# A convolution cut into single taps, an expert choice in four parts, and PSUM places opened earlier, in the last stage of a two-layer kernel

## The chip, the cores and the metric

The kernel runs on one core of a Trainium2 chip, in one launch, in fp32 throughout. The metric is the device time of an execution in microseconds; each kernel has the median of several executions, and one more execution is taken with the hardware profiler. All rows below are from that profiled execution.

The engines are named as the profile names them: PE (matmuls; PEld are its weight loads), DVE (VectorE), ACT (ScalarE), POOL (GpSimd) and SP (which issues DMAs). A matmul writes its result to PSUM, which is used here in eight places of 128 x 512 fp32; DVE or ACT reads it from there and so frees the place.

## What is computed

Two layers on `x` (2 x 1024 tokens of 256), with a context of 2 x 77 tokens. Every part is added to `x`.

```python
x = x + L0_xattn(ctx, layernorm(x))      # context and tokens as keys, 16 heads of 64
x = x + L0_ffn(layernorm(x))             # 8 experts of width 1024, 2 per token, layernorm behind
x = x + L1_xattn(layernorm(x), ctx, ctx) # 16 heads of 16 over 77 keys, causal mask
x = x + L1_ffn(layernorm(x))             # below
```

The change lies in the last line. With `h` for the normalized tokens it is

```python
scores = sigmoid(h @ Wr)                      # 8 choices, 4 of them expert networks
idx = top_k(scores + router_bias, 2)
cw = scores at idx, divided by their sum, 0 elsewhere
routed = sum over e < 4 of cw[:, e] * ((silu(h @ Wg[e]) * (h @ Wu[e])) @ Wd[e])
routed += (cw[:, 4] + cw[:, 6]) * h + cw[:, 7] * relu(h)
shared = conv(h, conv_w) + conv_b             # per channel, 4 taps back in time
out = x + routed + shared
```

## The kernel before

The whole is one program of some 25,000 instructions, written out without loops at run time. The order of each engine's instructions is the order in which the Python code issues them (`manual_schedule`), and every engine takes its own queue strictly in that order. So an instruction that waits holds up all behind it on its engine.

The last stage runs through **steps** k = 0 to 49. Steps 0 to 31 are the attention of the second layer: step k scores one tile of 128 tokens for one half of the heads (`score` on PE, `soften` on DVE and an Exp on ACT), and in step k + 1 its result is turned on PE (`turn_step`) and copied out by ACT. Steps 0 to 19 are woven into the last experts of the first layer (two steps in each of their slots 29 to 38); steps 20 to 49 stand alone. `step(k)` issues, in this order: `pre` (projections, turns back, divides of tiles), the scores, `mid` (attend), the turns of the step before, soften. After it the lists `rest`, `fill` and `after` of this k are run, each in the order in which things were put into it.

The last feed-forward part is done by `Mix` for four **blocks** of 512 tokens. For a block, with k = 8 * blk + 13:

- `measure` (fill, k): mean and variance of four tiles on DVE, and the power -0.5 on POOL.
- `values` (fill, k + 1): nb on DVE, then four ACT instructions that write the normalized tiles.
- `turns` (fill, k + 2): eight PE transposes, two ACT copies.
- `choose`, in three parts (fill k + 3, after k + 3, fill k + 4): 16 matmuls of 8 columns and an Exp; then 8 small DVE instructions, which end with the first choice; then 14 more (lines 200 to 206 and 1481 to 1489), which give `cw`.
- four experts, two steps each, from step 19 on: `up` (rest, first step) has 8 matmuls of 512 columns into two PSUM places and a Tanh (in the last block a Silu) on ACT; its `product` on DVE is put into `after` of that step. `down` (rest, second step of the next expert) has 8 matmuls into two places, and DVE adds the four tiles of them, times `cw`, to `xr` (line 1584).
- `copies` (fill, second steps of the first two experts): four ACT and four POOL instructions for `h` and relu of `h`.
- the convolution: `convolve_first` (fill, second step of expert 0: 19, 27, 35, 43) has two ACT passes with the first tap; `convolve(c)` (fill, first steps of experts 1 and 2) has three taps on DVE for half c of the channels; `convolved` (rest, both steps of expert 3) turns the result with PE and adds it on DVE (line 1531).

The experts of blocks 0 to 3 begin at steps 19, 26, 34 and 42 (the two steps of the very first fall together).

The profile's starts of some steps on PE: step 18 at 1520.6 us, 22 at 1551.9, 23 at 1557.5, 24 at 1567.3, 31 at 1616.0, 33 at 1632.1, 34 at 1637.9, 40 at 1660.4, 42 at 1669.1.

PSUM in this stage: `ps_t` has three places that all turns, projections and small matmuls take in turn. `ps_h` has two, for `up`. `ps_o` has one, for `attend` and for the first two tiles of `down`. The last two places hold the scores (`ps_s`). While `ps_x` is None, the last two tiles of `down` take a place of `ps_t`. At step K3 = 42 the scores' places are given up, and `ps_x` is opened in them, with one place for every third matmul result of `up` and one for the last two tiles of `down`. Its tiles wait for the readers of the tile that was in the place before (`reuse_waits="tile"`).

```python
ups[0] += 1
pool = ps_x if ps_x is not None and ups[0] % 3 == 0 else ps_h
```

## Time and profile before

| | us |
|---|---|
| median of 3 executions | 1699.35 (1698.52 to 1704.48) |
| profiled execution | 1698.73 |
| its span, from the first to the last instruction | 1696.9 |
| PE busy in it | 1631.6 |
| DVE busy | 1092.3 |
| ACT busy | 708.4 |
| POOL busy | 853.0 |
| one tap of the convolution (line 1521), 24 of them | 0.74 to 1.30, median 1.04 |
| one ACT pass of the first tap (line 1508), 8 of them | 0.80 |
| one addition of `down` on DVE (line 1584), 64 of them | 0.48 |

How to read the views: the list of waits gives, for an engine and a line, what ended its idle time, then the us in total, the number of times and the longest. The timeline gives the start and length of an instruction or a run of like ones, in us, and in brackets the idle time before it with what ended it. The chain of waits gives start, length and instruction along the chain that ended last. The table by stretches gives the busy us of each engine, with the granted clock of PE behind them (1.00 is full speed).

### The profile page before, as it was taken

The page shows a single profiled execution, that of the slowest core. Times are in us where ns is not written, and L with a number is a line of the kernel's source. Part 1 is how long each engine was busy: PE and PEld are TensorE (multiplying, and loading weights), DVE is VectorE, ACT ScalarE, POOL GpSimd, SP SyncE. Part 2 cuts the span into 40 slices and gives each one's busy share as a digit, 9 for nine tenths or more (in the row PEclk, how much of TensorE's full clock was granted, in tenths as well). Part 3 has the DMA queues.
Part 4 walks back from the last instruction along what each step waited for, and adds up shares of the span by engine and source line. Part 5 has one row for each costly group of instructions (what it writes and reads, how often), then busy time and mean ns, then how long its engine had stood idle before and what let it go on. Part 6 is the DMA issues. An engine that isn't in the chain of part 4 may idle for free.

```text
span 1696.9 us, 25161 instructions
## 1 busy us (share of the span) xinstructions
PE 1631.6 (96%) x9368; PEld 1048.2 (62%) x9368; DVE 1092.3 (64%) x2169; ACT 708.4 (42%) x1405; POOL 853.0 (50%) x538
## 2 busy tenths in 40 slices
PE   8998999999999999999999999989999999999998
PEld 4544555555555555565555555457899987886655
DVE  5766766666666666767767776664522266666777
ACT  1544444444544444444443444451222135445542
POOL 1277656775676666755776766823040143222112
PEclk8999999999999999999999999999999999999999
DMA  3011222222211210000000000018888987530000
GB/s 120 25 50 63 75 68 69 75 69 69 75 69 63 81 69 7 7 20 1 13 13 7 7 20 29 1 50 304 308 282 297 325 291 224 166 99 20 13 13 25
DMA packets 124910, 151.95 MB, mean 90 GB/s; under 512 B 13259, under 2 KB 112757, under 8 KB 124789
## 3 DMA queue, kind: packets, MB, share of 16 engines
q1 hardware_dynamic: 80032, 102.18, 18.2%
q10 hardware_dynamic: 41685, 39.77, 6.7%
q0 software_dynamic: 3072, 8.39, 1.4%
q8 instruction: 75, 1.23, 0.3%
q14 instruction: 46, 0.38, 0.1%
HBM read 105.10 MB, written 45.22 MB: 89 GB/s over the span
## 4 chain that ended last, share of the span: by engine, by line
PE 72%; DVE 13%; ACT 6%; POOL 6%; issue 2%; DMA 1%; ACTq 0%; DVEq 0%; POOLq 0%
PE sc L758 13%; PE ptr L810 12%; PE po L835 8%; PE ph L1258 8%; PE po L1277 7%; PE pqk L688 6%; POOL pa L792 5%; DVE nm L768 5%; ACT pa L769 4%; PE pv L664 3%; PE py L703 3%; PE pg L1540 2%; PE ptr L1356 1%; PE sb L733 1%; ACT pT L124 1%
## 5 line engine op out<-in xcount | busy, mean ns | idle before, releaser
L792 POOL TENSOR_SCALAR pa<-pa,f 128x1024 f32<-128x1024 f32 x244 | 694.9, 2865 | 360.5 <-ACT pT L124 258.1
L769 ACT ACTIVATE pa<-sc,nm 128x1024 f32<-128x1024 f32 x256 | 282.9, 1109 | 427.6 <-DVE nm L768 424.5
L768 DVE TENSOR_REDUCE nm<-sc 128x1 f32<-128x1024 f32 x256 | 301.2, 1218 | 136.2 <-PE sc L758 136.2
L810 PE MATMUL ptr<-ident,pa 128*128 128x128 f32 x2048 | 285.3, 278 | 26.7 <-DVE kT L128 6.2
L810 PEld LDWEIGHTS ptr<-ident,pa 128*128 128x128 f32 x2048 | 224.9, 141 | 110.1 <-issue 61.4
L835 PE MATMUL po<-pT,v 128*64 128x512 f32 (+1 forms) x1152 | 262.6, 598 | 0.0
L758 PE MATMUL sc<-kT,qT 64*128 64x512 f32 x1024 | 257.1, 621 | 0.0
L128 DVE COPY pT<-ptr 128x512 f32<-128x512 f32 x256 | 175.4, 688 | 100.3 <-PE ptr L810 97.0
L124 ACT COPY pT<-ptr 128x512 f32<-128x512 f32 (+1 forms) x320 | 177.5, 587 | 135.2 <-PE ptr L810 131.8
L835 PEld LDWEIGHTS po<-pT,v 128*64 128x64 f32 (+1 forms) x1152 | 78.5, 136 | 153.8 <-issue 148.7
L1258 PE MATMUL ph<-xT,w 128*128 128x128 f32 x1248 | 150.0, 277 | 2.3 <-DVE xT L128 1.5
L1258 PEld LDWEIGHTS ph<-xT,w 128*128 128x128 f32 x1248 | 146.3, 194 | 5.2 <-DVE xT L128 2.2
L758 PEld LDWEIGHTS sc<-kT,qT 64*128 64x128 f32 x1024 | 89.2, 187 | 84.1 <-issue 80.8
L1277 PE MATMUL po<-w,hT 128*128 128x256 f32 x624 | 141.1, 379 | 0.0
L1277 PEld LDWEIGHTS po<-w,hT 128*128 128x128 f32 x624 | 115.5, 190 | 14.1
L1271 DVE TENSOR_SCALAR hT<-ph,bs 128x128 f32<-128x128 f32 x156 | 43.9, 344 | 102.5 <-PE ph L1258 95.3
L162 POOL TENSOR_TENSOR rstd<-ve,neghalf 128x1 f32<-128x1 f32 (+2 forms) x45 | 31.9, 710 | 152.2 <-DVE ve L155 128.9
L1269 ACT ACTIVATE hT<-ph,bs 128x128 f32<-128x128 f32 x156 | 44.3, 367 | 114.1 <-PE ph L1258 102.4
L1015 POOL DMA_INDIRECT yt<-tab_y,pos x32 | 31.5, 984 | 95.2 <-PE po L1277 80.9
L688 PE MATMUL pqk<-kvT,wk 128*128 128x512 f32 (+1 forms) x192 | 73.5, 513 | 0.0
L664 PE MATMUL pv<-wv,kvT 128*128 128x256 f32 (+1 forms) x288 | 69.2, 382 | 2.9 <-DVE pB L744 2.3
L664 PEld LDWEIGHTS pv<-wv,kvT 128*128 128x128 f32 (+1 forms) x288 | 52.3, 185 | 25.1 <-issue 16.2
(258 smaller groups left out, 1830.1 us busy)
## 6 DMA issues: line engine op xcount, KB each, us to landing
w<-in_L_ffn_W_dram SPq DMA_DIRECT2D x78, 1024.0 KB, 6.8
tab_x<-zero ACTq DMA_DIRECT2D x32, 512.0 KB, 3.2
tab_y<-zero ACTq DMA_DIRECT2D x32, 512.0 KB, 3.2
xs<-tab_x SPq DMA_DIRECT2D x39, 128.0 KB, 6.3
tab_y<-y ACTq DMA_DIRECT2D x39, 128.0 KB, 5.4
wq<-in_L_xattn_Wq_dram SPq DMA_DIRECT2D x8, 256.0 KB, 2.8
wk<-in_L_xattn_Wkv_dram SPq DMA_DIRECT2D x8, 256.0 KB, 2.9
wv<-in_L_xattn_Wkv_dram SPq DMA_DIRECT2D x8, 256.0 KB, 3.7
```

The costliest lines, as they stand in the source:

```text
L124: nc.scalar.copy(dst, src)
L128: nc.vector.tensor_copy(dst, src)
L664: nc.tensor.matmul(ps[:r, n * GC : (n + 1) * GC], kvT[b][:, c, kt * P : kt * P + r], groups[G]["v"][:, c, :], start=(c == 0), stop=(c == 1),)
L688: nc.tensor.matmul(ps[:, : n1 - n0], groups[G][nm][:, c, p * P : (p + 1) * P], kvT[b][:, c, n0:n1], start=(c == 0), stop=(c == 1),)
L758: nc.tensor.matmul(sc[j][:, n * 512 : (n + 1) * 512], U.qT[j * DH0 : (j + 1) * DH0, q0 : q0 + P], U.kT[j * DH0 : (j + 1) * DH0, n * 512 : ...
L768: nc.vector.tensor_reduce(U.nm[:, 0, r : r + 1], sc[j], AX.X, ALU.max, negate=True)
L769: nc.scalar.activation(U.pa[t][:, j, :], sc[j], AF.Exp, bias=U.nm[:, 0, r : r + 1], accum_out=U.l[:, 0, r : r + 1])
L792: nc.gpsimd.tensor_scalar_mul(pa, pa, f)
L810: nc.tensor.transpose(ps[:, n * P : (n + 1) * P], U.pa[t][:, j, kt * P : (kt + 1) * P], ident)
L835: nc.tensor.matmul(U.po[j * DH0 : (j + 1) * DH0, :], v[:r, kt, h0 : h0 + DH0], U.pT[j][:r, kt, :], start=(kt == 0), stop=(kt == NKT - 1),)
L1258: nc.tensor.matmul(ps[:, n * TB : (n + 1) * TB], w1[:, c, f * P : (f + 1) * P], xT[:, c, :], start=(c == 0), stop=(c == 1),)
L1277: nc.tensor.matmul(ps[:, :D], hT[:, f, :], w2[:, f, :], start=(f == 0), stop=(f == NF - 1))
```

## The change

Three things are changed, all in the last stage.

1. `choose` has four parts: its third part ends behind the second choice (line 206), and the six instructions from line 1481 on become a fourth part. They are put into `fill` at k + 3, `after` k + 3, `fill` k + 4 and `fill` k + 5.
2. `convolve(c, k)` does one tap. `convolve_first` moves to `fill` of k + 4 (steps 17, 25, 33, 41), and the six taps go one by one into `after` of k + 5 to k + 10 (18 to 23, 26 to 31, 34 to 39), in the last block two each into `after` of 42, 43 and 44. They are put ahead of the experts' products in the same list. In the last block `convolved` moves from expert 3 to expert 2, that is from steps 48 and 49 to 46 and 47.
3. `ps_x` is opened at step 33 and not 42, two steps behind the last scores (step 31).

```diff
@@ Mix.choosing
             yield next(two)
-            next(two)
+            yield next(two)
             nc.vector.tensor_tensor(sel, sel, sg, ALU.mult)
@@ Mix
-        def convolve(self, c):
+        def convolve(self, c, k):
             cv = self.cv[:, c, :]
             src = hT2[self.b][:, c, self.off - KC + 1 : self.off + 512]
-            for k in range(1, KC):
-                nc.vector.scalar_tensor_tensor(
-                    cv, src[:, k : k + 512], cw1[:, c * KC + k : c * KC + k + 1], cv, ALU.mult, ALU.add
-                )
+            nc.vector.scalar_tensor_tensor(
+                cv, src[:, k : k + 512], cw1[:, c * KC + k : c * KC + k + 1], cv, ALU.mult, ALU.add
+            )
@@ the lists of a block
         k = begins(2 * blk + 1) + 9
-        for n, f in enumerate((m.measure, m.values, m.turns, m.choose, m.choose)):
+        for n, f in enumerate((m.measure, m.values, m.turns, m.choose, m.choose, m.choose)):
             put(fill, k + n, f)
         put(after, k + 3, m.choose)
+        put(fill, k + 4, m.convolve_first)
+        for n in range(2 * (KC - 1)):
+            put(after, k + 5 + (n if blk < NBLK - 1 else n // 2), m.convolve, n // (KC - 1), n % (KC - 1) + 1)
@@ the lists of an expert
-        if e == 0:
-            put(fill, k[1], m.convolve_first)
-        if e in (1, 2):
-            put(fill, k[0], m.convolve, e - 1)
-        if e == 3:
+        if e == (3 if blk < NBLK - 1 else 2):
             for i in range(4):
                 put(rest, k[i // 2], m.convolved, i)
@@ the last steps
         for k in range(K1, K3 + 8):
-            if k == K3:
+            if k == begins(NT // 2 - 1) + 5:
                 spare.close()
                 ps_x = ctx.enter_context(tc.tile_pool(name="d_ps_x", bufs=1, space=PSUM, reuse_waits="tile"))
```

## The prediction

> **What bounds the kernel.** I read the page's first two parts, then the list of PE's waits from 1500 us on, since the edits lie behind step 16 of the last stage (step 18 starts at 1520.6 us), then the timeline of each engine there, and the clock in short stretches.

> ```profile
> PE 1631.6 (96%) x9368; PEld 1048.2 (62%) x9368; DVE 1092.3 (64%) x2169; ACT 708.4 (42%) x1405; POOL 853.0 (50%) x538
> ```

> TensorE is busy 96% of the span, and the edits leave its instructions as many and as long as they are. So they can move only the gaps between them. PE's waits from 1500 us to the end:

> ```profile
> PE py L1406 <- ACT hT L124: 2.9, 2, 2.1
> PE pt L1063 <- DVE xr L1584: 1.6, 1, 1.6
> PE pt L1063 <- ACT h L1056: 1.4, 1, 1.4
> PE pg L1540 <- DVE sl L1562: 1.2, 2, 0.7
> PE pt L1446 <- ACT h L1432: 1.1, 4, 0.6
> PE po L1576 <- ACT raw L1376: 0.7, 1, 0.7
> PE pt L1446 <- DVE at L1387: 0.7, 1, 0.7
> PE ptr L1356 <- ACT aT L1400: 0.6, 2, 0.3
> PE po L1576 <- DVE at L1387: 0.6, 1, 0.6
> PE pn L1382 <- DVE xr L1584: 0.5, 1, 0.5
> ```

> The second number is the times, the third the longest. With two rows of 0.3 and 0.2 behind these they sum to 11.8 us: that is all the change can fill, 0.7%, and the 6.5 us of the first, the fourth and the last four rows are what the edits touch. The chain of waits shows what is behind the first row:

> ```profile
> 1559.32 0.91 DVE cv L1521
> 1560.25 1.11 DVE cv L1521
> 1561.38 1.10 DVE cv L1521
> 1562.49 0.61 DVE sl L1562
> ...
> 1566.08 0.72 ACT pr L1346
> 1566.80 0.48 ACT hT L124
> 1567.32 1.93 PE py L1406 x4
> ```

> Three taps stand ahead of DVE's product, divide and soften; ACT's Exp waits for soften, the copy of the turned tile waits behind Exp, and PE for the copy's buffer. The gap has a second price:

> ```profile
> 1566.00:1568.00 2.00, 0.68 (x2) 0.59 (x3) 2.00 (x6) 1.68 (x3) 0.00 (x0) 0.88 0.00 0
> 1568.00:1570.00 2.00, 2.00 (x7) 1.29 (x8) 1.76 (x7) 0.23 (x1) 0.46 (x1) 0.50 0.00 0
> 1570.00:1572.00 2.00, 2.00 (x13) 1.18 (x12) 1.90 (x6) 0.51 (x2) 0.81 (x2) 0.77 0.00 0
> ```

> The last number but two is the granted clock: half speed for about 3.5 us. From start to start the projection takes 1.72 us there (0.86 at 1598.74), the turn back 0.57 (0.31), the scores 1.33 (0.72): 0.86 + 0.26 + 0.61 = 1.7 us lost. From 1500 us on only 1504 to 1512 reads low as well (0.76, 0.81), with hardly a wait: there choose's 16 matmuls of 8 columns stand at 1504.31, and the next 16 matmuls of the hidden layer take 3.61 us and not 1.95. The same 8-column matmuls at 1575.74, 1630.38 and 1664.38 cost no clock.

> **The change part by part.** Times are those of before. All 24 taps stay; one costs 0.75 us alone and 1.10 beside POOL's additions (the rows of L1521 have both); the stage's DVE sum is unchanged.

> *Block 0, steps 17 to 23.* The two ScalarE passes of the first tap (pitch 1.42 us) move from step 19 to 17, ahead of normal of tile 12. The last six instructions of choose (1.17 us) move to step 18, so the shift for that tile comes 1.17 us earlier, at 1518.3. ACT is free of Exp at 1518.24; 1518.24 + 1.42 = 1519.66, against a start of 1519.64 now. PE's 1.44 us wait stays: 0, bounds -1.2 and +0.3. The taps of steps 18 to 20 fall into DVE's idle times (3.21, 2.67 and 4.74 us): 0.

> *Step 23 (the chain above).* The tap of step 21 now stands behind measure and ahead of divide and soften of step 22: 0.85 us, between 0.75 and 1.10. Exp, the four values of block 1 and the copy of the turned-back tile come that much later, and PE's 0.32 us wait for that copy grows to 1.17. Behind that, step 22 has one tap of 1.10 in place of three (pitch 3.18): DVE is 3.18 - 0.85 - 1.10 = 1.2 us earlier at the product, and so are divide, soften, Exp and copy: the projection starts at 1566.1 in place of 1567.32. PE's waits there, 0.68 + 2.10, become about 1.0, in the last part alone. Whether the clock then drops no row says: bounds 0 and 1.7 us. I take that it stays up, as at 1583.5 to 1585.1 (one wait of 1.62 us) and at 1655 to 1660.4 (1.7 us in pieces), where it read 1.00; where it fell, 2.78 of the 3.43 us before were idle. Sum 1.2 + 1.7 = 2.9. The next wait, 1.62 us at 1585.10, is for a buffer behind product, addition and soften, with no moved tap before it (DVE is idle 2.62 us before the convolution's turn): it stays.

> [...]

> *Step 31, the same place in block 1.* Waits of 0.33, 0.57 and 0.76 us, no clock lost. The tap ahead of soften makes the first about 1.2; DVE is again 1.2 us ahead afterwards, which ends the second, and the third becomes 0.25, because PE's own turns end at 1623.5. The projection starts 0.6 us earlier (bounds -0.3 and +1.2).

> *Own PSUM places from step 33.* The second output bank of the experts leaves the three shared banks: the 0.53 us wait of divide (L1382) goes. A third input bank: PE takes each bank again after three and not two, so the two waits of 0.65 and 0.57 us on DVE's L1562 go. The 0.71 us wait for raw stays, as attend and the first output bank still share one. Opening the places waits for the last scores, read by soften at 1623.1, 9 us before: 0.

> *Steps 34 to 40.* Behind the 0.53, DVE has choose's last part (1.17) and a tap (0.75) ahead of the product of step 34; the turn back of tile 15 waits 0.1 us for it. DVE's addition of step 37 starts at 1650.3 (1651.01 now), and measure ends 0.6 earlier. The tap of step 37 lies in the 1.14 us that DVE waits for POOL's power, so nb is 0.4 earlier, at 1655.75, and so are ACT's values and PE's turns. With the 0.65 that is no longer waited for: up of expert 3 starts at 1659.35 in place of 1660.40, a gain of 1.05 (bounds 0 and 1.7).

> *Block 3, steps 40 to 49.* Here DVE is nearly full: from 1664.36 to the end it idles 0.58, 0.67 and 1.38 us.

> ```profile
> 1674.70 0.68 DVE L1560 TENSOR_TENSOR hid<-sl,pg 128x512 f32<-128x512 f32 x1
> 1675.30 1.65 DVE L1584 SCALAR_TENSOR_TENSOR xr<-po,cw,xr 128x256 f32<-128x256 f32 x4
> 1677.62 2.67 DVE L1521 SCALAR_TENSOR_TENSOR cv<-hT,cw,cv 128x512 f32<-128x512 f32 x3 [0.67 <-ACT cv L1508]
> ```

> Two taps (1.85 us) now stand before the first product, which ends at 1677.2 and not 1675.3, and the addition behind it frees the output bank at 1677.95. PE, 0.57 earlier, wants it at 1677.15: a new wait of 0.85 us. Steps 43 and 44 have four taps (3.8 us), and the second product ends at 1682.8; PE, which asks for it at 1683.6 behind the convolution's turn, doesn't wait. The convolution is added two steps earlier, so DVE's end has two sets of four additions (1.65 each) without 0.74 between: from PE's last matmul at 1692.9, DVE ends at 1693.45 against 1693.65. Gain 0.2 with the 0.57 in it, bounds -1.5 (all taps at 1.10, PE's wait twice) and +1.2 (no wait). The output DMA of 3 us behind it is the same.

> **Sum.** 2.9 + 0.6 + 1.05 + 0.2 = 4.75 us. The profiled execution took 1698.73 us for a span of 1696.9; less 4.75 that is 1694.0. It lies 0.6 below the median of the three runs, so of the median I forecast 1699.35 - 4.75 = 1694.6.

> **Rivals.**
> 1. *The clock still falls at step 23.* 2.15 us of waits remain there, 1.17 of them new in place. For it: no row gives the threshold. Against: no wait over 1.2. Without the 1.7: 1696.3. Chance 0.20.
> 2. *The taps ahead of soften take back what those behind it give,* or the places opened are not taken in the order that I assume: steps 23 and 31 give nothing, what is left is 1.05 + 0.2: 1698.1. For it: DVE has no idle time from 1551.3 to 1573 in any order. Chance 0.12.
> 3. *Slower: the clock falls at new places.* Each shortened wait becomes two short ones, and if about 2 us of small gaps or of thin matmuls in a stretch can drop the clock, it falls at steps 23, 31, 39 and 45. The price of each fall is 1.7 us by both rows above; one is there already, so three new ones cost 5.1 against the 3.05 won without the clock: 1699.35 + 2.05 = 1701.4. It decides from the second new fall on. For it: the fall at 1504, nearly without a wait. Against it: the stretches with 1.6 to 1.7 us of waits read 1.00, and so do three of the four with the thin matmuls. Chance 0.13. [...]
> 4. *More is won:* with DVE ahead, the waits of 1.62 and 0.71 us shrink too and block 3 takes no wait: 4.75 + 2.3 + 0.9 = 7.95: 1691.4. Chance 0.12.
> The forecast itself, with 1692.5 to 1696.5 around it: 0.43.

> From these cases, and since one of the three runs of before lies 5 us above the others, the range is 1690.5 to 1701.5; it takes in all but a part of the third rival. A measurement of this kernel tells about 0.5% (8.5 us) from no change: faster by more needs nearly every wait gone, 0.06; slower by more needs two dearer things than any I found, 0.04; within it 0.90.

> **What would show it.** Right: in the stretch before the third projection of block 1's steps (1567 now) PE's longest wait under 1.3 us and the clock 1.00; no wait of L1540 for L1562; none of L1382 for L1584; the wait for the turned-back tile near 1.2 at steps 23 and 31; a new wait of L1576 of about 0.9 in block 3. Wrong: a granted clock under 0.9 in a stretch of 4 us behind 1512; a wait of L1576 or L1530 over 1.5 us in block 3 (DVE is then the bound there); PE's 1.4 us wait at 1520 grown by over 0.3 (the first tap's passes then block ACT).

## The result, and the profile after

| | before | after |
|---|---|---|
| median of 16 executions each, us | 1698.95 (1697.13 to 1704.48) | 1695.87 (1693.14 to 1698.49) |
| ratio of the times | | 0.9974 (95%: 0.9966 to 0.9981) |
| profiled execution, us | 1698.73 | 1697.47 |
| its span, us | 1696.9 | 1695.8 |
| from the turn of step 18 to the last instruction, us | 176.61 | 172.15 |

The ratio is that of the mean times (1695.74 and 1700.17 us), a gain of 4.4 us (3.2 to 5.8); the medians lie 3.1 us apart. The two spans differ by only 1.1 us, and that is no contradiction: in code that is the same in both kernels, ahead of step 18, the profiled execution of after ran 3.36 us later (PE starts the first turn of step 18 at 1520.29 us before and at 1523.65 after). The last row of the table leaves that out. I call it the **stretch**, and all comparisons below use it: it went down by 4.46 us. Spans are given to 0.1 us, so a stretch is good to about 0.05 us.

New line numbers in after: the taps are L1520, `convolved` L1529 and L1530, `up` L1539, the product L1561 and L1562 (last block: L1559), `down` L1575, its additions L1583.

The first part of the page of after: PE is as busy as before, to 1.2 us of 1631.6. What moved is the idle time.

```profile
PE 1630.4 (96%) x9368; PEld 1047.9 (62%) x9368; DVE 1088.8 (64%) x2169; ACT 709.1 (42%) x1405; POOL 851.8 (50%) x538
```

DVE is busy 3.5 us less with as many instructions. The groups of the tile cv, first of before and then of after (shortest, median and longest ns, first and last start), show where it is shorter:

```profile
L1521 DVE SCALAR_TENSOR_TENSOR cv<-hT,cw,cv x24: 740/1040/1303, 1543.0 to 1684.7; 128x512 f32<-128x512 f32 x24
```

```profile
L1520 DVE SCALAR_TENSOR_TENSOR cv<-hT,cw,cv x24: 736/745/1297, 1529.2 to 1679.2; 128x512 f32<-128x512 f32 x24
```

Spread out, more of the taps lie away from POOL's additions, and the median tap has the length that a tap has alone: POOL's additions to `xr` (lines 1499 and 1502) overlap 15 of the 24 taps before, by 0.55 us or more, and 5 in after (four more by 0.04 us at most). The taps that they don't touch take 0.74 to 0.75 us in both traces.

PE's waits of after from 1500 us to the end (us in total, times, longest):

```profile
PE pt L1063 <- DVE xr L1583: 1.6, 1, 1.6
PE pt L1446 <- ACT h L1432: 1.5, 4, 1.0
PE pt L1063 <- ACT h L1056: 1.4, 1, 1.4
PE ptr L1356 <- DVE at L1387: 1.1, 1, 1.1
PE po L1575 <- DVE xr L1583: 1.1, 1, 1.1
PE ptr L1356 <- ACT aT L1400: 1.0, 1, 1.0
PE py L1406 <- ACT hT L124: 0.8, 2, 0.6
```

The row for hT, 2.9 us before, is down to 0.8. The rows of `up` waiting for the product and of divide (L1382) waiting for an addition are gone. Four rows are new or larger: 1.1 and 1.0 us for the turned-back tile at steps 31 and 23, 1.0 us (0.6 before) for the first normalized tile at step 39 (L1446 for L1432), and 1.1 us of `down` (L1575), for its bank, in block 3. The chain of waits of after at step 23:

```profile
1563.35 0.75 DVE cv L1520
1564.10 0.61 DVE sl L1561
...
1567.70 0.72 ACT pr L1346
1568.42 0.48 ACT hT L124
1568.95 1.13 PE py L1406 x4
```

One tap is left ahead of the product instead of three. The table by stretches of after, the same place:

```profile
1566.00:1568.00 2.00, 2.00 (x14) 1.77 (x13) 1.97 (x5) 0.69 (x2) 0.70 (x2) 1.00 0.00 0
1568.00:1570.00 2.00, 1.41 (x9) 1.02 (x8) 1.90 (x6) 1.38 (x3) 0.00 (x0) 1.00 0.00 0
1570.00:1572.00 2.00, 2.00 (x16) 1.42 (x15) 1.85 (x6) 0.73 (x2) 0.72 (x1) 1.00 0.00 0
```

The granted clock stays at 1.00 where it read 0.50 before. In after it reads 1.00 from the turn of step 18 to PE's last matmul (1691.63 us).

The stretch, cut at instructions that both kernels have (us):

| part | before | after | difference | predicted |
|---|---|---|---|---|
| turn of step 18 to the projection (L1406) at step 23's end | 47.03 | 45.30 | -1.73 | -1.2 |
| that projection to the next one | 10.13 | 8.51 | -1.62 | -1.7 |
| to the projection behind step 31 | 46.92 | 46.22 | -0.70 | -0.6 |
| to `up` of expert 3 at step 40 | 36.03 | 34.98 | -1.05 | -1.05 |
| to the end (block 3) | 36.50 | 37.14 | +0.64 | -0.2 |
| sum | 176.61 | 172.15 | -4.46 | -4.75 |

### The profile page after: what moved, and what is told of

The parts are those of the page before. It is cut to its first block, busy times and chain, and to the rows that moved or that the text cites. A ratio compares the mean times of both kernels' runs of the same rounds, so it can differ in the third digit from the quotient of the medians.

```text
span 1695.8 us, 25167 instructions
## 1 busy us (share of the span) xinstructions
PE 1630.4 (96%) x9368; PEld 1047.9 (62%) x9368; DVE 1088.8 (64%) x2169; ACT 709.1 (42%) x1405; POOL 851.8 (50%) x538
## 4 chain that ended last, share of the span: by engine, by line
PE 71%; DVE 12%; ACT 7%; POOL 6%; issue 2%; DMA 1%; SPq 0%; ACTq 0%; DVEq 0%; POOLq 0%
PE sc L758 13%; PE ptr L810 12%; PE po L835 8%; PE ph L1258 7%; PE po L1277 7%; PE pqk L688 6%; POOL pa L792 5%; DVE nm L768 5%; ACT pa L769 4%; PE pv L664 3%; PE py L703 3%; PE pg L1539 2%; PE ptr L1356 1%; PE sb L733 1%; ACT pT L124 1%
## 5 line engine op out<-in xcount | busy, mean ns | idle before, releaser
L124 ACT COPY pT<-ptr 128x512 f32<-128x512 f32 (+1 forms) x320 | 177.5, 587 | 135.4 <-PE ptr L810 131.9
L162 POOL TENSOR_TENSOR rstd<-ve,neghalf 128x1 f32<-128x1 f32 (+2 forms) x45 | 33.7, 749 | 152.6 <-DVE ve L155 126.8
```

The costliest lines, as they stand in the source:

```text
L124: nc.scalar.copy(dst, src)
```

## The experiments

My theory was the prediction's sum: the taps give the two gains at step 23 and a part of those at step 31, the places those from step 33 on, choose's fourth part nothing, and the taps of block 3 lose. The rivals: that the places or the choice carry the gain, and that the taps set ahead of soften cost as much as they win. Runs of one group share a chip with their own runs of before; ratios are to those. b1, e3 and c1 were one execution each, so no ratio stands for them. The intervals of a1, a2 and a3 overlap, so how the gain splits between the parts is read from the stretch, of one profile each. No kernel here leaves out a part of the computation.

| kernel | stretch expected | measured (before 176.61) | ratio to before |
|---|---|---|---|
| after | | 172.15 | 0.9974 [0.9966, 0.9981] |
| a1, places only | 175.1 | 175.04 | 0.9982 [0.9969, 0.9994] |
| a2, taps only | 173.0 | 172.84 | 0.9977 [0.9963, 0.9992] |
| a3, choose only | 176.6 | 177.74 | 0.9986 [0.9974, 0.9998] |
| a4, after without block 3's taps | 171.1 | 170.71 | 0.9959 [0.9946, 0.9972] |
| b1, block 0's taps only | 173.3 | 173.32 | |
| b2, after, no tap ahead of those softens | 170.85 | 172.74 | 0.9970 [0.9958, 0.9983] |
| b3, after, block 3's taps later | 170.55 | 170.62 | 0.9953 [0.9937, 0.9970] |
| d1, after, first tap later | 172.15 | 172.19 | 0.9967 [0.9954, 0.9980] |
| e2, after, block 1's choice later | 170.75 | 171.60 | 0.9968 [0.9955, 0.9981] |
| e1, all four together | 168.2 | 170.74 | 0.9942 [0.9924, 0.9959] |
| e3, e1 without the choice | 169.6 or 171.2 | 169.59 | |
| c1, two taps at step 22 | 174.5 | 174.95 | |

### The three parts alone

**a1_places_only**: before, with the places opened at step 33.

```diff
-            if k == K3:
+            if k == begins(NT // 2 - 1) + 5:
```

> Kernel before with one edit: the experts' own PSUM places are opened at step 33. Stretch from the first turn of step 18 (line 1063) to the last instruction: 176.6 us before, 172.15 after. My theory: the wait of divide for the second output bank (0.53) and the two waits for L1562 (0.65 and 0.57) go, the last only in part since DVE is nearly full in block 3: stretch 175.1 (174.8 to 175.5), time 1.5 us under before; step 23 keeps its wait of over 2 us and the half clock. Rival 'the places carry most of the gain': 3 us or more. Rival 'DVE is the bound behind step 33, so the places bring nothing': under 0.5 us.

The stretch is 1.57 us shorter, about half of it up to `up` of expert 3 at step 40 and half behind. PE's waits on the product are gone, as in after. Divide's wait for an addition (0.53) is gone too, but nothing is won by it: PE comes earlier to the turn back of step 34 and waits 0.86 us there (L1398 for L1387), since DVE does that divide behind choose's last instructions. At step 23 the clock falls as before (0.64 in the 4 us from 1572).

**a2_taps_only**: after, with choose in three parts and the places opened at 42.

> Kernel before with the convolution of after (first tap at k + 4, single taps, last block's convolved with expert 2), choice in three parts, places opened at step 42. My theory: step 23 gives 3.3 us (1.7 of order, 1.6 of clock), step 31 0.7, the 0.65 us wait for L1562 at step 40 goes, the divide's 0.53 stays, and block 3 loses 1.1 (a new wait of down for its bank): 3.6 us under before (2.5 to 4.5), stretch 173.0. Rival 'the taps only move the wait': under 1 us. Rival 'the clock falls by its own phase and not by the wait': 1.6 us less than mine, 2.0, with a granted clock under 0.9 in a 4 us stretch behind 1516.

The stretch is 3.77 us shorter, and the clock reads 1.00 up to PE's last matmul. So the taps carry most of the change. But 3.77 and 1.57 make 5.34, and after has 4.46: on top of the taps the places, together with choose's fourth part, which a2 lacks as well, are worth 0.7 and not 1.57. The traces say where the rest is. With the taps alone, PE's wait of 0.65 us for the product at step 40 goes too, as one tap and not three stands ahead of that product; only 0.37 us are won by it, because the turns at step 39 come 0.44 us later. There POOL's power (L162), behind which nb and the normalized tiles stand, takes 1.45 us with a tap beside it (in after) and 1.02 without (in before). And the bank wait of block 3 is 0.3 us here and 1.08 in after. `up` still waits 0.6 us for the product ahead of it in a2; in after PE comes to the bank so much earlier and waits there.

The 0.7 us that are left lie in steps 32 to 36, where a1 wins nothing. In after DVE does the divide of step 34 (1639.53 us) ahead of choose's last six instructions (from 1639.88), and a1's wait of 0.86 us isn't there. So the places need choose's fourth part here. That is read from the order of the instructions; taps and places with choose in three parts were not run.

**a3_choose_only**: before, with choose in four parts.

```diff
-            next(two)
+            yield next(two)
...
-        for n, f in enumerate((m.measure, m.values, m.turns, m.choose, m.choose)):
+        for n, f in enumerate((m.measure, m.values, m.turns, m.choose, m.choose, m.choose)):
```

> Kernel before with the choice in four parts and nothing else. My theory: in after this gain is hidden by the first tap's ACT passes; alone, the shift of tile 12 in step 17 comes 1.17 us earlier and ACT is free, so PE's wait of 1.4 us for line 1056 ahead of step 18 falls to about 0.3: time 1.1 us under before, and the stretch counted from the first turn of step 18 stays 176.6. Rival 'the parting does nothing': wait 1.4, time as before. Rival 'a later cw delays the copies': over 0.5 us slower.

PE's wait before step 18 falls from 1.44 to 0.16 us, as expected: alone, the split is worth 1.28 us, ahead of the stretch. In after the two passes of the first tap stand in that place on ACT. ACT in the timeline of after:

```profile
1521.60 1.51 ACT L1508 ACTIVATE cv<-hT,cb,cw 128x512 f32<-128x512 f32 x2
1523.01 0.59 ACT L1056 ACTIVATE h<-xr,nb,rstd 128x256 f32<-128x256 f32 x1
```

L1056 is what PE's 1.45 us wait for. That part of the prediction (0 for both together) is shown. The stretch itself missed: 177.74. The waits at step 23 are those of before, but the clock stayed low for longer (6.8 us, and 3.41 before). Table by stretches of a3, the last number but two is the clock:

```profile
1566.00:1568.00 2.00, 1.41 (x3) 1.18 (x4) 1.86 (x6) 1.02 (x3) 0.00 (x0) 0.53 0.00 0
1568.00:1570.00 2.00, 2.00 (x8) 0.97 (x6) 1.86 (x6) 0.37 (x1) 0.72 (x1) 0.50 0.00 0
1570.00:1572.00 2.00, 2.00 (x10) 1.65 (x9) 1.90 (x6) 0.47 (x1) 0.55 (x1) 0.50 0.00 0
```

From projection to projection it takes 11.53 us, against 10.13 before and 8.51 in after. One and the same pattern of waits cost 1.6 us of clock in one execution and 3.0 in another.

**b1_first_block_only**: before, with the single taps in block 0 alone.

> Kernel before with the convolution moved as in after in block 0 alone (first tap at step 17, one tap in each of steps 18 to 23); choice in three parts, places at 42, blocks 1 to 3 as before. My theory (a wait of over 2 us at step 23 lets the clock fall): PE's longest wait at the projection of step 24 falls from 2.1 to 0.6 us, the clock stays 1.00 there, and the stretch from the first turn of step 18 falls from 176.6 by 3.3 to 173.3. Rival 'the clock falls by its own phase': it falls there all the same, stretch 174.9. Rival 'the later blocks take it back': 176.

Measured 173.32: 3.3 us, all that the change wins at step 23, come from block 0's six taps, and the clock reads 1.00. PE's last wait there is 0.59 us as in after, and all the waits of the later steps are before's. The mean clock of every execution points the same way beyond the profiles: on one chip 0.9912 over 26 of before, 0.9916 and 0.9918 in a1 and a3, where the clock fell at step 23, and 0.9923 and 0.9928 in a2 and a4, where it did not. One spell of 3.41 us at half clock is 0.0010 of it, and the means are uncertain by 0.0003 to 0.0007.

### What the taps ahead of soften cost

**b2_not_before_soften**: after, with the tap of step 21 moved to 20, and that of 29 to 28.

```diff
+        at = ((0, 1, 2, 2, 4, 5), (0, 1, 2, 2, 4, 5), (0, 1, 2, 3, 4, 5), (0, 0, 1, 1, 2, 2))[blk]
...
-            put(after, k + 5 + (n if blk < NBLK - 1 else n // 2), m.convolve, ...)
+            put(after, k + 5 + at[n], m.convolve, ...)
```

> Kernel after, but the taps of steps 21 and 29, which stand between measure and soften, are put into steps 20 and 28 (two taps there). My theory (a tap ahead of soften costs its pitch of 0.67 us at Exp, values and the copy that PE waits for): PE's waits of 1.0 and 1.1 us for the second turn of steps 23 and 31 fall to 0.3 and 0.4, stretch 172.15 - 1.3 = 170.85, time 1.3 under after. Rival 'the gain is lost at the next wait, for the copy behind soften': waits of line 1406 for L124 grow instead, stretch within 0.3 of 172.15.

The order gave most of what I expected: the waits of 1.0 and 1.1 us for the turned-back tile became 0.3 and 0.7, and 1.04 us were won over steps 23 and 31, not 1.3. The stretch is longer nevertheless, as the clock fell at another place, behind PE's wait of 1.63 us in step 25, which is no different in before and after. Table by stretches of b2:

```profile
1588.00:1590.00 2.00, 2.00 (x12) 1.18 (x12) 1.77 (x11) 0.61 (x3) 0.00 (x0) 0.73 0.00 0
1590.00:1592.00 2.00, 2.00 (x8) 1.58 (x8) 1.95 (x4) 1.54 (x3) 0.73 (x1) 0.50 0.00 0
```

That cost 1.65 us. Its ratio (0.9970) is not to be told from after's. So the second rival's tap costs about 0.5 us at each place, and that is a part of what the taps win there and not all of it.

**c1_two_taps_at_22**: after, with block 0's last tap moved from step 23 to 22, so that two taps stand ahead of the product.

> Kernel after, but block 0's last tap moves from step 23 to 22, so two taps stand ahead of the product and soften before the projection of step 24. My theory: PE's wait of 0.6 us there grows by one tap to 1.3, on top of the 1.0 for the copy, 2.3 us within 4; the stretch grows by 0.7 to 172.9 if the clock holds and by 2.4 to 174.5 if it falls. I take the fall, since the waits' sum comes near that of before (3.1). Rival 'only one long wait lets it fall': 172.9 with 1.00.

I was wrong here. The wait grew more than I thought, and the clock did not fall at step 23. PE in the timeline of c1:

```profile
1569.71 0.66 PE L1356 MATMUL ptr<-ident,pr 128*77 128x128 f32 x4 [0.99 <-ACT aT L1400]
1570.20 1.98 PE L1575 MATMUL po<-wd,hid 128*128 128x256 f32 x8
1572.02 1.04 PE L1446 MATMUL pt<-ident,h 128*128 128x128 f32 x8
1574.79 1.13 PE L1406 MATMUL py<-l1wo,aT 128*128 128x256 f32 x4 [1.74 <-ACT hT L124]
```

The projection takes 1.13 us, as in after with the clock at 1.00 (1.93 in before, at 0.50). Nearly as much was waited for as before (2.73 against 2.78 us), but with 3.3 us of matmuls between the two waits and not 0.66. In this execution the clock fell at 1664 instead (0.66 and 0.50), behind waits of 1.02 and three of 0.16 us in step 39, where after, with the same waits, reads 1.00. Of the 2.8 us that c1 lost to after, 1.15 are the order and 1.65 that fall.

### Block 3

**a4_last_block_old**: after, with the last block's convolution as in before.

> Kernel after, with the convolution of the last block as in before (first tap at 43, three taps at 44 and at 46, convolved at 48 and 49). My theory: the two taps ahead of the first product and of the addition that frees the output bank cost block 3 its 1.08 us wait, so here PE's wait of down for its bank in block 3 is under 0.2 and the stretch 171.1, 1.0 us under after, 5.4 under before. Rival 'DVE's sum bounds block 3 in any order': the wait goes but the end stays, within 0.3 of after's stretch 172.15. Rival 'the earlier convolved is worth more than the wait': 0.5 slower than after.

**b3_last_block_later**: after, with the last block's taps two each in 43, 44 and 45, and `convolved` in 48 and 49 as in before.

> Kernel after, but the taps of the last block stand in steps 43, 44 and 45 (two each, so behind the first product and the addition that frees the output bank) and its convolved in 48 and 49 as in before. My theory: PE waits nowhere in block 3; stretch 172.15 - 1.6 = 170.55, DVE's last addition no longer follows PE's last matmul by more than 1 us; a little under the kernel with the old order in block 3 (170.71). Rival 'DVE's sum bounds block 3': wait moved to line 1529 or 1575, stretch 172.

Both lose the 1.08 us wait and 1.4 to 1.5 us of the stretch, so the taps of step 42 and the earlier `convolved` of block 3 cost that much together. In a4 and b3 PE has no wait at all from `up` of expert 3 to the end. The two edits were not tried apart. Read from the timelines of after and b3, the bank wait holds PE up by 1.24 us from start to start, and 0.27 us more go at the last two `down`, which stand back to back in after.

### What is left in the order

**d1_first_tap_later**: after, with block 0's first tap in step 18 and not 17.

```diff
-        put(fill, k + 4, m.convolve_first)
+        put(fill, k + (4 if blk else 5), m.convolve_first)
```

> Kernel after, but the two ACT passes of block 0's first tap stand in step 18 and not 17, so behind normal of tile 12. My theory (they hide what the choice in four parts gives, shown alone with a wait of 0.16): PE's wait of 1.45 us for line 1056 falls to 0.2, time 1.2 under after; the stretch counted from that turn is the same, 172.15, unless ACT's Exp of step 18 comes late (bound +0.4). Rival 'the wait only moves to the next turn or to step 18': time within 0.5 of after.

PE's wait before step 18 is 0.2 us, from the projection to the turn it takes 5.7 us and not 7.0, and the stretch behind it is unchanged (172.19). Here choose's fourth part is worth what a3 showed.

**e2_choice_behind_down**: after, with block 1's second part of choose behind the additions of `down`, in step 25.

```diff
-        put(after, k + 3, m.choose)
+        put(after, k + (4 if blk == 1 else 3), m.choose)
```

> Kernel after with the later place of choose's second and third part in block 1 alone. My theory: the 1.62 us wait of line 1063 falls to 0.2, stretch 172.15 - 1.4 = 170.75, the rest as in after. Rival as above: the stretch stays within 0.4 of 172.15.

The wait of 1.62 us became 0.53, but a wait of 0.3 us for qT (L1382) became 0.8: half of it was given back, and 0.55 us stay.

**e1_all_together** (b3, d1, b2's taps and e2's choice) and **e3_together_old_choice** (the first three of them):

> Kernel after with four edits: taps of the last block in steps 43 to 45 and convolved in 48 and 49 (1.5 us shown); block 0's first tap in step 18 (1.2 shown, ahead of the stretch); the taps of steps 21 and 29 in 20 and 28 (1.0 shown where the clock held); in block 1 the second part of choose behind the down of step 25 and its third part in after of 25, so that the addition which frees the shared bank comes 1.5 us earlier. My theory: PE's wait of 1.62 us for L1583 falls to 0.2, the clock then holds at 1588, stretch 172.15 - 1.5 - 1.0 - 1.4 = 168.2 and a ratio to before of about 0.994. Rival 'DVE is behind in block 1 whatever the order': the 1.6 us wait is replaced by one of divide or soften in step 26 or 27, stretch 169.6.

> The first kernel of this set without the later choice, so with the 1.62 us wait at step 25. If the clock held, the stretch is 169.6. [...] Rival 'moving the taps of steps 21 and 29 is what lets it fall': 171.2.

e3 has the shortest stretch of all, 169.59 us, 7.0 below before, with the clock at 1.00 up to PE's last matmul; with the 1.3 us won ahead of it that is 8.3 us in this one execution. e1 should have been another half a us shorter; in its profile the clock fell at 1664 to 1668 (0.57). Over its six executions e1 has the lowest ratio, 0.9942: 9.9 us (7.0 to 13.0) faster than before, and its interval lies wholly below after's, though it overlaps those of a4, b2, b3, d1 and e2. e3 has one execution, so which of e1 and e3 is faster is open.

## Why the prediction was right, and where it was not

The prediction has the sign and the sum (4.75 against 4.4 by the ratio and 4.46 by the stretch), within the 0.5% to which it gave 0.90. In part that is luck, as its terms are further off and cancel: step 23 gave 0.45 us more than I wrote, and block 3 0.84 less.

**Block 0, steps 17 to 23: right.** The cost of 0 held: a3 and d1 show that choose's split alone would have given 1.3 us, and that the first tap takes them.

**Step 23: right, 2.9 predicted, 3.35 measured.** The order gave 1.73 and not 1.2. I had set the two taps at 0.85 and 1.10 us; their pitch was 0.67 and 0.76. The first has only POOL's power beside it; the second still has two of POOL's additions beside it and took 0.83 us. The waits are 0.99 and 0.59 us, where I wrote about 1.17 and 1.0. The clock gave 1.62 (predicted 1.7). That the clock would stay up was a choice between 0 and 1.7, made by two stretches with 1.6 to 1.7 us of waits that read 1.00. Here it came out so in all eleven profiles with the shorter or more scattered waits, but in b2 it fell behind 1.63 us and in c1 behind 1.02 and three of 0.16, so such stretches are not safe.

**Step 31: right, 0.6 and 0.70.** The first wait is 1.1 us where I wrote 1.2, but DVE's divide (L1387) ends it and not the copy of the turned-back tile.

**Own places and steps 34 to 40: the sum is right, 1.05 and 1.05, its terms are not.** I wrote 0.40 us by the earlier nb and 0.65 by the product's wait. Counted from the projection behind step 31, the turns at step 39 come 0.24 us earlier, and from there to `up` it takes 0.81 less. `measure` does start 0.68 us earlier, but the tap that I put into DVE's wait for POOL's power made the power longer, 1.45 us for 1.02, and the sum had no term for that. And causes overlap that I had only added: a2 shows the 0.65 us wait go by the taps as well, and a1 shows that the 0.53 of divide is not won by the places alone.

**Block 3: the mis-sized term.** Predicted 0.2 won, measured 0.64 lost. DVE and PE in the timeline of after:

```profile
1672.86 2.03 DVE L1520 SCALAR_TENSOR_TENSOR cv<-hT,cw,cv 128x512 f32<-128x512 f32 x2
1674.81 0.68 DVE L1559 TENSOR_TENSOR hid<-sl,pg 128x512 f32<-128x512 f32 x1
1675.41 1.65 DVE L1583 SCALAR_TENSOR_TENSOR xr<-po,cw,xr 128x256 f32<-128x256 f32 x4
```

```profile
1676.33 1.99 PE L1575 MATMUL po<-wd,hid 128*128 128x256 f32 x8 [1.08 <-DVE xr L1583]
...
1687.64 3.99 PE L1575 MATMUL po<-wd,hid 128*128 128x256 f32 x16
```

The mechanism is the one I gave: two taps ahead of the first product, the addition behind it frees the bank, PE waits for it. Two sizes were off, and one wait was missing from the sum. The wait is 1.08 us and not 0.85. The end: I let DVE finish 0.55 us behind PE's last matmul, since nothing but the additions is left, and it is 0.91 (1692.54 against 1691.63; before, 0.97). DVE stood idle for 0.36 us there, waiting for PE: the first two of the last four additions start at 1690.80 us, when the matmuls into their place have ended (1690.77), and the other two at 1691.67, 0.04 behind PE's last matmul. The last 0.27 us lie with PE, whose last 16 matmuls take 3.99 us against 1.73 + 1.99 = 3.72 before. Before, 0.44 us of `convolved` stood between these two `down`; in after the second comes to its bank before DVE has added the first, and the weight loads wait 0.5 us for L1583 there. So the earlier `convolved` brought nothing and cost this. The three make up the difference: 0.23 + 0.36 + 0.27 = 0.86 against 0.84 us.

**The rivals.** 1 (the clock falls at step 23 all the same): in none of the eleven profiles with other waits than before's. 2 (taps ahead of soften take it back): b2 puts it at about 0.5 us at each of the two places, a quarter (step 23) and two fifths (step 31) of what the order would win without. 3 (slower, the clock falls at new places): its price is right, 1.65 us in b2 and in c1 (and once 3.0, in a3, at the old place); of its places step 39 showed, and step 25, which it did not name, but one fall or none came to a profile, and it needed two. The falls at 1664 in c1 and e1 came behind waits of 1.0 and three of 0.16 us; eight other profiles with those waits read 1.00. 4 (more is won): not with this order; e1 shows it was to be had.

**Of the signs**, the first three showed as written, with the hT wait at 0.6 us; the waits for the turned-back tile were 0.99 and 1.1, the bank wait 1.08 for 0.9. None of those for "wrong" came: the low clock of after at 1508 to 1516 us (0.68 and 0.90 in pieces of 4 us) is that of before at 1504 to 1512, the same instructions 3.4 us later.

## What to carry to other kernels

Where one engine takes its queue in order, price a moved instruction by its pitch at its new neighbours, not at its old ones: the same tap took 0.74 to 0.75 us away from POOL's additions, and beside them in before mostly 1.1 and up to 1.30. Idle time is not free either, where the engine waited for gets slower by what is put there, as POOL's power did (1.45 us for 1.02). An engine whose last input is another's last matmul can't end earlier by being free sooner (in after DVE, with less to do at the end, ended 0.91 us behind PE, and in before 0.97), so the work to move out of the end is what stands behind that matmul. And when an execution's span is noisier than the change (5.4 us in one pair of runs, against 4.4), compare the time between two fixed instructions of the trace: it resolved terms of 0.1 us and showed where a part gave back what another had won.

## What the runs showed of the hardware that was not expected

The same waits don't always give the same clock. From the turn of step 18 to PE's last matmul, in the 14 profiles:

| place | PE's waits ahead, us | clock fell in |
|---|---|---|
| step 23 | 0.3, 0.7 and 2.1 within 6.7 us | 3 of 3 (before, a1, a3) |
| step 23 | 1.0 + 0.6, 1.0 + 1.7 or 0.3 + 0.7 | 0 of 11 |
| step 25 | 1.6 in one piece | 1 of 12 (b2) |
| step 39 | 1.0 and three of 0.16 | 2 of 10 (c1, e1) |

Each fall cost 1.6 to 1.7 us, once 3.0. Ahead of the stretch the clock fell at choose's 16 matmuls of 8 columns in step 16, nearly without a wait (0.23 us), in 6 of the 14. The half clock begins there 1.76 us behind the first of these matmuls in before (1506.07 for 1504.31) and 1.73 in after (1509.40 for 1507.67).

In the 3.41 us ahead of its fall PE was idle for 2.6 us in before, 2.4 in a1, 2.3 in a3, 1.6 in b2 and 1.5 in c1. But the wait ahead of b2's fall stands in eleven other profiles that read 1.00 at step 25, and the waits ahead of those of c1 and e1 in eight that read 1.00 at step 39. What tells these executions apart, and how much idle time lets the clock fall, was not shown.

Even identical code differs in time: on one chip the turn of step 18 started at 1528.35 us in c1 and at 1533.70 in e2, whose edits lie behind it. The mean granted clock of the two profiled executions was 0.992 in c1 and 0.989 in e2: over some 1704 us that is an estimated 5.1 us more lost in e2 (3.4 to 6.8, as the means are rounded), though c1 alone lost 1.65 us to a fall behind step 18. So falls of the clock can account for the 5.35 us; how many lay ahead of step 18 and what each of them cost was not measured.
